# Loads, weight sums and powers of a fused gated block, placed anew

## The chip, the cores and the metric

The kernel runs on one core of a Trainium2 chip. The metric is the device time of one execution in microseconds (us), lower is better. A profile of a single execution shows its span, which is a little shorter than the time. Five engines work side by side, each in the order of its own instructions: TensorE (PE in the profile, PEld for its weight loads), VectorE (DVE), ScalarE (ACT), GpSimd (POOL) and SyncE (SP). SP computes nothing; it issues DMAs.

## The reference

```
x    = x + tanh(g_xattn) * (0.6 * sigmoid(si + sj + b) + 0.4 * layernorm(x))   # si, sj: products of ctx with two rows of W
y    = layernorm(x)
gate = silu(bitlinear(y, w1));  up = bitlinear(y, w2)
x    = x + tanh(g_ffn) * bitlinear(gate * up, w3)

bitlinear(x, w): xn = x * rsqrt(mean(x*x) + 1e-6)
                 xq = round(xn * 127 / max|xn|), scaled back, for each row
                 wq = clip(round(w / mean|w|), -1, 1) * mean|w|
                 xq @ wq.T
```

x is 4 x 512 x 512, ctx 4 x 512 x 128, w1 and w2 are 1408 x 512, w3 is 512 x 1408, all in float32. The mean of |w| runs over a whole weight, so no block of a weight can be rounded before all of it has been read and summed.

## The kernel before, in words

The 2048 rows of x are 16 tiles of 128 rows, numbered 0 to 15, four to each batch. A weight lies in blocks: w1 and w2 in four blocks of 128 x 1408 (704 KB each), w3 in three blocks of 128 x 1536 and one of 128 x 1024. A list of words, `ORDER`, is the program: a loop at the end of the kernel (L576) takes word after word and emits that step. An engine runs its steps in the order of the list, and waits by semaphores for what a step reads and for buffers that it overwrites; nothing reorders them later. So a step that waits holds up all later steps of its own engine, and on SP a DMA that waits holds up every later load, even one that could go at once.

A word is a step's name, a tile or weight number, after a dot the block, and a letter for the engine (a ScalarE, v VectorE, p GpSimd). The steps by their names:

- SP: `x4` loads a tile (tiles 0 to 3) or a pair of tiles, `ctx1` a batch's context, `w1.0` a weight block; `t4` turns an integer 128 x 512 tile with a transposing DMA (L432), `T4` the 128 x 1408 one (L504), `O4` writes a result (L542).
- Attention and first norm: `pi`, `pj` (PE) with `si`, `pjs` (ACT) make the scores; `st` (DVE) statistics, `la`, `lb`, `lc` the layer norm's factors; `th` (ACT) the tanh, `at` (DVE) the sum, `ce` the centring, `am`, `an` (DVE) the largest value and its inverse, `sq` (ACT) the squares, `r` the rounding to int8 range, `dq` (POOL) the factor that undoes it. Tiles 0 to 3 are turned by PE (`pt`), the others by `t`; `un` widens the result to float16, and PE reads that.
- Weights: `A` sums |w| of a block (L241 on ACT, L243 on DVE), `tot` adds the sums over the rows on PE (L247), `M` is the mean (DVE), `R` scales and rounds a block, `C` clips it. `A3.2a` is block 2 of w3 on ACT.
- Products: `G1.0` is tile 1 times block 0 of w1, `U1.0` the same with w2; `G6` does all four blocks. One tile's G, or its U, is 12 matmuls. `SI` (silu, ACT) empties a G, `ST` (DVE) a U. G and U share two PSUM buffers (`ps_gu`), so a product waits for the emptying of the one before the last. `AM`, `AN`, `SQ`, `QU`, `T`, `W` quantize and turn the product, `D` is its product with w3 (11 matmuls), `DQ`, `S`, `O` scale, add and write.
- Small ones: `bp`, `up` spread a scalar parameter over the rows and apply tanh, `cg`, `cc`, `mr`, `os` compute constants of a few values (`mr` is four GpSimd instructions, L480 to L484), `wu5` lets PE run 5 idle matmuls. Small PE results (`pi`, `pj`, `bp`, `tot`, `pt`, `po`) share two other PSUM buffers (`ps_o`).

Before the list starts, ScalarE's own DMA queue gets the attention rows, the first context (`load_ctx(act, 0)`), two scalars, the block w1.3 (`load_w(act, 1, W1_FIRST)`) and the last scalar; then come ScalarE's table load and its first instructions. Inverse square roots are a power of -0.5 on GpSimd, followed by one Newton step (four small instructions, L218 to L221).

Of the kernel before, what the change touches and what calls it, by code (L numbers as in the profile page):

```python
# [32 lines left out]
ORDER = """
x1 bp1 x3 x0 st3 up1 st1 bp0 up0 st0 la0 A1.3a cg lb0p pi0 si0 x2 x4 w1.0 st2 ctx1 st5 pj0 th1 th0
at1 ce1v th3 A1.0a th2 at0 ce0v sq0 x6 w1.2 cc am0 an0 sq1 A1.2a wu5 pi1 si1 la2 lb2p am1 an1 st6
pj1 pjs1 at2 ce2v at3 w1.1 A1.1a w2.2 A2.2a r0p st4 wu4 pt0 wu6 tot1 st7 am2 M1 r1p un0v R1.1v C1.1
R1.0a C1.0 wu3 pt1 R1.2v C1.2 un1a wu6 G1.0 G1.1 G0.0 dq0 w2.3 w2.0 A2.3v G0.1 G1.2 A2.0a w2.1
R1.3p C1.3 A2.1a tot2 an2 ce3a M2 R2.0v R2.2v th6 C2.0 C2.2 R2.1a C2.1 G0.2 G0.3 am3 G1.3 SI1 ctx2
pi2 lc0 pj2 SI0 U1.0 U1.1 U1.2 x8 st9 sq2 th7 la4 lb4p U0.0 U0.1 R2.3p mr at6 C2.3 U1.3 at7 U0.2
U0.3 x10 an3 si2 pjs2 r2p pt2 th5 ce6a ST1 ctx3 pi3 sq3 un2a G2.0 ST0 w3.2 r3p pt3 w3.0 G2.1 G2.2  # L40
G2.3 ce7a am7 sq7 un3a G3.0 G3.1 G3.2 G3.3 A3.0a dq2 lc4 SI2 at5 an7 U2.0 U2.1 U2.2 U2.3 r7p th4
am6 an6 r6p SI3 st8 st11 U3.0 U3.1 U3.2 U3.3 t6 fx1p st10 ce5a si3 at4 ce4v w3.1 sq5 am4 an4 am5
an5 un6v sq4 sq6 bp2 la8 lb8p dq4 ST2 th10 pj3 t7 un7a w3.3 ST3 th11 at11 A3.2a AM2 AN2 G6 SI6 AM1
AM0 th8 r5p AN1 ce11a G7 SI7 U7 ST7 at8 am11 an11 t5 up2 A3.3a r4p U6 ST6 t4 un4a G4 lc8 A3.1a tot3
QU2p QU1p lc2 th9 at9 un5a G5 ce8a T1 SI4 ce9a fx0p W1v T2 at10 ce10v sq9 r11p t11 AN0 un11a U5 SI5
M3 R3.1p sq10 sq8 am10 am9 an9 an10 r10p am8 an8 r9p r8p sq11 dq8 ST5 x12 st13 U4 ST4 t9 un9v R3.3v
C3.3 C3.1 x14 SQ1 st14 st15 pjs3 th13 R3.2p th12 G11 SI11 t8 un8a U11 ST11 st12 R3.0a C3.0 th15 W2v
fx2p QU0p C3.2 os la12 SQ0 lb12p t10 AM6 AN6 QU6p th14 T0 un10v AM3 G9 SI9 at14 ce14v SQ2 fx3a AN3
G8 am14 D1 fx11p SI8 D2 fx6a an14 at15 at12 SQ7 at13 U8 ce13v T6 W0a DQ0 S1 SQ3 QU3v ST8 G10 DQ2
AM4 fx4p ce15a sq15 S2 T3 r14p t14 am13 an13 SI10 D0 r13p t13 AM7 U10 fx7p W6v AN4 QU4p SQ5 U9 S0  # L50
am15 W3a D3 fx9a ST10 ce12a am12 T4 AN7 un13v lc12 fx13v fx14p D6 S3 sq14 un14a G14 O0 sq12 sq13
dq12 ST9 AM10 SQ6 DQ6 W4a SQ4 SI14 QU7p T7 AM5 AN5 SQ10 an15 r15p G13 SI13 D4 U14 AN10 S6 QU5p AM8
U13 T5 AN8 an12 O6 r12p t12 SQ8 W7a D7 fx8a AM9 AN9 QU9v T9 SQ9 ST14 un12v G12 W5v fx15a fx10p O1
DQ4 SQ14 AM14 DQ14 QU8p S4 AN14 QU14v D5 ST13 SQ11 AM11 W9a AN11 S7 U12 SI12 D9 fx5p DQ8 t15 DQ10
un15a S5 G15 ST12 T14 SQ13 QU10v W14a D14 SI15 T8 T10 S9 O9 QU11p AM12 AN12 W8v AM13 T11 AN13 S14
O3 SQ12 U15 D8 W10a D10 QU12p T12 ST15 AM15 QU13p S8 DQ12 AN15 QU15v O14 S10 W11a D11 fx12a T13
W12v D12 W13v T15 O2 O8 S11 O11 O4 O5 O10 SQ15 S12 D13 O12 W15v S13 O7 DQ15 D15 S15 O13 O15
"""


# [1 line left out]
def flamingo_gated_kernel(  # L62
# [72 lines left out]
    def load_ctx(eng, b):  # L135
        eng.dma_start(ctxs[b], ctx_t[:, b * S : (b + 1) * S])

    def load_w(eng, i, k):
        if i < 3:
            eng.dma_start(wf[i][k], (w1t, w2t)[i - 1][k * P : (k + 1) * P, :])  # L140
        else:
            f0, f1 = k * W3S, min((k + 1) * W3S, NH)
            eng.dma_start(
                wf[3][k].rearrange("p (f d) -> p f d", d=D),
                w3t[f0 * P : f1 * P, :].rearrange("(f p) d -> p f d", p=P),
            )
# [10 lines left out]
    mhalf = const.tile([P, TB], F32, name="mhalf")  # L157
# [54 lines left out]
        dve.reciprocal(c_inv, c_sig)  # L212
        dve.scalar_tensor_tensor(c_abs, c_inv, -1.0, c_inv, ALU.mult, ALU.max)

    def newton(eng, r, y, w, n, tag):

        p = small.tile([P, n], F32, tag=f"{tag}_p", name=f"{tag}_p")
        eng.tensor_tensor(p, y, y, ALU.mult)  # L218
        eng.tensor_tensor(p, p, w, ALU.mult)  # L219
        eng.tensor_scalar(p, p, -0.5, 1.5, ALU.mult, ALU.add)  # L220
        eng.tensor_tensor(r, y, p, ALU.mult)  # L221

    def rsqrt(eng, w, n, tag):

        y = small.tile([P, n], F32, tag=f"{tag}_y", name=f"{tag}_y")
        pool.tensor_tensor(y, w, mhalf[:, :n], ALU.pow)
        r = small.tile([P, n], F32, tag=f"{tag}_r", name=f"{tag}_r")
        newton(eng, r, y, w, n, tag)
        return r
# [394 lines left out]
```

## Time and profile before

| | us |
|---|---|
| median of 3 runs (154.28 to 154.74) | 154.52 |
| the profiled execution's own time | 154.62 |
| its span | 152.8 |
| PE busy in the span | 137.5 |
| DVE, ACT, POOL busy | 127.9, 114.2, 101.5 |

The profiled execution is 0.10 us above the median, and 1.8 us of it lie outside the span. A view's times are counted from the span's start. In a view of instructions in order of time, a row gives start, length, engine, line, operation, output and inputs, and in brackets how long the engine was idle before it and what ended that. A row that merges several instructions has their number behind an x.

PE's first product starts at 26.1 us and its last ends at 149.1 us. DMA runs at about 400 GB/s until 31 us, and is then idle for long stretches.

### The profile page before, as it was taken

To read this page: it belongs to the slowest core of one execution; us is meant where nothing else is said; L and a number is where in the kernel's file an instruction comes from. 1 tells how busy PE (TensorE), PEld (TensorE's weight loads), DVE (VectorE), ACT (ScalarE), POOL (GpSimd) and SP (SyncE) were. 2 spreads that over 40 slices of the span, in tenths; PEclk is the share of its full clock that TensorE was granted. 3 is DMA by queue.
4 is the path that set the end of the run, shared out by engine and by line. 5 is a ranking of instruction groups with operands and counts; after the bars stand their busy time and mean duration, and the time that the engine had idled before them with its cause. 6 is when DMAs were issued, how large, how long until landed. Compare 5 with 4: busy or idle time off the path is not lost.

```text
span 152.8 us, 2189 instructions
## 1 busy us (share of the span) xinstructions
PE 137.5 (90%) x659; PEld 67.5 (44%) x659; DVE 127.9 (84%) x226; ACT 114.2 (75%) x167; POOL 101.5 (66%) x214
## 2 busy tenths in 40 slices
PE   5379776799999989999989999999999999999990
PEld 2273433354644434544444444444444444444440
DVE  0384999999999789999899979999995999868521
ACT  0166998879999399999799998888989990928000
POOL 3058473959787865638898978687993788983400
PEclk9999999999999999999999999999999999999998
DMA  5999999940004921672905404351099382599894
GB/s 138 288 417 407 417 417 373 389 180 2 2 0 63 349 42 31 131 186 78 206 0 99 94 0 94 71 101 67 5 193 215 80 166 48 144 178 232 227 381 183
DMA packets 37300, 25.57 MB, mean 167 GB/s; under 512 B 30247, under 2 KB 30248, under 8 KB 37288
## 3 DMA queue, kind: packets, MB, share of 16 engines
q1 hardware_dynamic: 36992, 24.45, 56.5%
q10 hardware_dynamic: 296, 0.98, 2.0%
q8 instruction: 5, 0.08, 0.2%
q14 instruction: 7, 0.06, 0.1%
HBM read 13.89 MB, written 4.19 MB: 118 GB/s over the span
## 4 chain that ended last, share of the span: by engine, by line
DVE 38%; POOL 21%; PE 17%; DMA 12%; issue 6%; ACT 3%; SPq 1%; POOLq 0%; DVEq 0%
PE po L531 12%; DMA x<-in_x_dram 6%; DVE f_am L487 6%; DMA q1t<-q 6%; DVE hs L475 5%; DVE st L346 4%; DVE x L368 4%; DVE am L387 4%; PE pu L463 3%; DVE wk L265 3%; POOL q L499 3%; POOL q L416 3%; POOL x L376 2%; PE pg L463 2%; DVE x L536 1%
## 5 line engine op out<-in xcount | busy, mean ns | idle before, releaser
L463 PEld LDWEIGHTS <-ht 128*128 128x128 f16 x384 | 37.4, 98 | 42.8 <-issue 3.8
L463 PE MATMUL pg<-w1q,ht 128*128 128x512 f16 (+1 forms) x192 | 40.3, 361 | 1.6 <-DVE w1q L268 0.9
L463 PE MATMUL pu<-w2q,ht 128*128 128x512 f16 (+1 forms) x192 | 39.8, 361 | 0.8 <-ACT hs L471 0.7
L531 PE MATMUL po<-w3q,qt 128*128 128x512 f16 x176 | 39.5, 379 | 0.1
L475 DVE SCALAR_TENSOR_TENSOR hs<-pu,a,hs 128x1408 f32<-128x1408 f32 x16 | 26.6, 1673 | 1.7 <-PE pu L463 1.5
L471 ACT ACTIVATE hs<-pg,a 128x1408 f32<-128x1408 f32 x16 | 22.7, 1423 | 5.4 <-PE pg L463 4.2
L531 PEld LDWEIGHTS <-qt 128*128 128x128 f16 x176 | 17.2, 98 | 20.5 <-issue 0.3
L487 DVE TENSOR_REDUCE f_am<-hs 128x1 f32<-128x1409 f32 x16 | 25.6, 1609 | 0.0
L495 ACT ACTIVATE junk<-hs 128x1408 bf16<-128x1408 f32 x16 | 21.9, 1367 | 0.1
L499 POOL TENSOR_SCALAR q<-hs,f_qs 128x1408 int16<-128x1408 f32 x11 | 15.8, 1442 | 4.0 <-DVE f_qs L492 3.6
L346 DVE BATCH_NORM_STATS2 st<-x 128x6 f32<-128x512 f32 x16 | 10.8, 676 | 6.0 <-DMA x<-in_x_dram 6.0
L536 DVE SCALAR_TENSOR_TENSOR x<-po,f_dq,x 128x512 f32<-128x512 f32 x16 | 11.8, 742 | 4.5 <-PE po L531 3.7
L511 ACT ACTIVATE qt<-qtk 128x1408 f16<-128x1408 int16 x8 | 11.0, 1373 | 5.6 <-PE po L531 3.0
L368 DVE SCALAR_TENSOR_TENSOR x<-x,sc,th_all 128x512 f32<-128x512 f32 x16 | 12.1, 766 | 3.6 <-POOL l_p L219 1.9
L387 DVE TENSOR_REDUCE am<-th_all 128x1 f32<-128x513 f32 x16 | 10.7, 674 | 0.1
L399 ACT ACTIVATE junk<-th_all 128x512 bf16<-128x512 f32 x16 | 10.0, 628 | 0.3
L171 PE MATMUL idle<-ones 128*128 128x512 f16 x27 | 8.6, 453 | 1.8 <-POOL ones L166 1.8
L241 ACT ACTIVATE junk<-hs 128x1408 bf16<-128x1408 f32 x7 | 9.6, 1375 | 0.7 <-DMA hs<-in_w1t_dram 0.6
L416 POOL TENSOR_SCALAR q<-th_all,qs 128x512 int16<-128x512 f32 x12 | 8.2, 693 | 1.2 <-DVE qs L396 0.8
L339 ACT ACTIVATE th_all<-ctx,si 128x512 f32<-128x512 f32 x12 | 8.5, 712 | 0.1
L522 POOL TENSOR_SCALAR f_w<-f_ss,kap 128x2 f32<-128x2 f32 (+1 forms) x9 | 3.9, 433 | 5.8 <-ACT junk L495 5.2
L376 POOL TENSOR_SCALAR x<-x,c_sig,sh 128x512 f32<-128x512 f32 x9 | 7.4, 817 | 0.1
(107 smaller groups left out, 180.7 us busy)
## 6 DMA issues: line engine op xcount, KB each, us to landing
out_dram<-x SPq DMA_DIRECT2D x16, 256.0 KB, 2.9
x<-in_x_dram SPq DMA_DIRECT2D x6, 512.0 KB, 7.4
hs<-in_w2t_dram SPq DMA_DIRECT2D x4, 704.0 KB, 11.8
w3f<-in_w3t_dram SPq DMA_DIRECT2D x3, 768.0 KB, 8.8
hs<-in_w1t_dram SPq DMA_DIRECT2D x3, 704.0 KB, 7.4
x<-in_x_dram SPq DMA_DIRECT2D x4, 256.0 KB, 5.0
...
```

The lines of the kernel that those rows point to most:

```text
L346: dve.bn_stats(st, xt(n))
L368: dve.scalar_tensor_tensor(xt(n), xt(n), col(sc, n), ths[n], ALU.mult, ALU.add, accum_out=col(ysum, n))
L387: dve.tensor_reduce(col(am1, n), th_all[:, th_slot[n], : D + 1], AX.X, ALU.max, apply_absolute_value=True)
L416: eng.tensor_scalar(q1s[n], ths[n], col(qs1, n), 127.0 * sign[n], ALU.mult, ALU.mult)
L463: pe.matmul(gus[tag, n][:, c0 : c0 + cn], hts[n][:, kk, :], wq[:, kk, c0 : c0 + cn], start=(kk == 0), stop=(kk == ND - 1),)
L471: act.activation(tts[n], gus.pop(("pg", n))[:, :H], AF.Silu, scale=col(a1, n))
L475: dve.scalar_tensor_tensor(tts[n], gus.pop(("pu", n))[:, :H], col(a1, n), tts[n], ALU.mult, ALU.mult)
L487: dve.tensor_reduce(col(f_am, n), hs[:, t_slot[n], : H + 1], AX.X, ALU.max, apply_absolute_value=True)
L495: act.activation(junk[:, :H], tts[n], AF.Square, accum_out=col(f_ss, n))
L499: eng.tensor_scalar(fq[n], tts[n], col(f_qs, n), 127.0, ALU.mult, ALU.mult)
L531: pe.matmul(po[:, :D], qt[:, f, :], w3q[:, f, :], start=(f == 0), stop=(f == NH - 1))
L536: dve.scalar_tensor_tensor(xt(n), pos.pop(n)[:, :D], col(f_dq, n), xt(n), ALU.mult, ALU.add)
```

## The change

- ScalarE's queue keeps only the attention rows and the three scalars. The first context and block w1.3 move to SP, as `ctx0` (the second load) and `w1.3` (the eleventh). `load_w(act, ...)` and `W1_FIRST` are gone.
- The Newton step is gone from all inverse square roots: `newton` is removed, `rsqrt` is one power on GpSimd. `lb` of the first four tiles goes to VectorE.
- The sum over the last block of w1 and of w2 is made in two halves (`A1.3`, `A1.4`, `A2.3`, `A2.4`), so these weights have five partial sums. Two of w1's are now made on VectorE.
- The clip can be given to an engine; all clips stay on VectorE.
- `ORDER` is new from the first word to the last. Among much else: second and third contexts are loaded ahead of most of w1; the idle matmuls between the first ones and the products go from 24 to 15; most centrings go to GpSimd; tile 2's `G` comes ahead of tile 0's and 1's `U`; the first int8 tile to be turned by DMA is 4 instead of 6, and on SP the loads `x12 w3.1 w3.2 w3.3` stand directly behind `t4`. `A3.2a` and `A3.3a` stand directly ahead of `un4a` on ScalarE.

```diff
 ORDER = """
-x1 bp1 x3 x0 st3 up1 st1 bp0 up0 st0 la0 A1.3a cg lb0p pi0 si0 x2 x4 w1.0 st2 ctx1 st5 pj0 th1 th0
-at1 ce1v th3 A1.0a th2 at0 ce0v sq0 x6 w1.2 cc am0 an0 sq1 A1.2a wu5 pi1 si1 la2 lb2p am1 an1 st6
-pj1 pjs1 at2 ce2v at3 w1.1 A1.1a w2.2 A2.2a r0p st4 wu4 pt0 wu6 tot1 st7 am2 M1 r1p un0v R1.1v C1.1
-R1.0a C1.0 wu3 pt1 R1.2v C1.2 un1a wu6 G1.0 G1.1 G0.0 dq0 w2.3 w2.0 A2.3v G0.1 G1.2 A2.0a w2.1
-R1.3p C1.3 A2.1a tot2 an2 ce3a M2 R2.0v R2.2v th6 C2.0 C2.2 R2.1a C2.1 G0.2 G0.3 am3 G1.3 SI1 ctx2
-pi2 lc0 pj2 SI0 U1.0 U1.1 U1.2 x8 st9 sq2 th7 la4 lb4p U0.0 U0.1 R2.3p mr at6 C2.3 U1.3 at7 U0.2
-U0.3 x10 an3 si2 pjs2 r2p pt2 th5 ce6a ST1 ctx3 pi3 sq3 un2a G2.0 ST0 w3.2 r3p pt3 w3.0 G2.1 G2.2
-G2.3 ce7a am7 sq7 un3a G3.0 G3.1 G3.2 G3.3 A3.0a dq2 lc4 SI2 at5 an7 U2.0 U2.1 U2.2 U2.3 r7p th4
-am6 an6 r6p SI3 st8 st11 U3.0 U3.1 U3.2 U3.3 t6 fx1p st10 ce5a si3 at4 ce4v w3.1 sq5 am4 an4 am5
-an5 un6v sq4 sq6 bp2 la8 lb8p dq4 ST2 th10 pj3 t7 un7a w3.3 ST3 th11 at11 A3.2a AM2 AN2 G6 SI6 AM1
...
+bp1 x1 st1 ctx0 x0 up1 cg st0 x2 st2 cc x3 st3 bp0 w1.0 up0 la0 lb0v ctx1 pi0 si0 pj0 th1 at1 ctx2
+th0 at0 wu5 pi2 th3 la2 lb2v w1.1 w1.2 ce1a th2 at3 am1 ce0p sq1 at2 an1 ce2p am0 an0 ce3p A1.2v
+w1.3 A1.3v A1.0a sq0 r0p si2 A1.1a am2 an2 pi1 si1 pj2 x4 A1.4a wu3 tot1 M1 st4 st5 x6 st6 pjs2
+w2.0 w2.1 w2.2 sq3 sq2 r1p pt1 R1.2a un1v wu1 pj1 R1.0p C1.0v C1.2v R1.1a C1.1v pjs1 th4 wu6 pt0
+un0v th5 A2.1a st7 G1.0 w2.3 A2.0a x14 G1.1 G0.0 G0.1 G0.2 G1.2 dq0 am3 an3 R1.3p C1.3v A2.3a G1.3
+r2v A2.2v la4 lb4p A2.4a ctx3 SI1 pt2 un2v at4 at5 tot2 M2 R2.0v C2.0v G0.3 x8 st9 st8 pi3 x10 st10
+r3p SI0 si3 R2.1a C2.1v R2.2a C2.2v dq2 R2.3p C2.3v th6 st11 at6 G2.0 G2.1 lc2 pt3 G2.2 un3a ce4p
+pj3 G2.3 U1.0 U1.1 U1.2 U1.3 ST1 am4 an4 w3.0 SI2 ce6p am6 mr AM1 A3.0a th7 r4p t4 sq6 ce5p am5 bp2
+up2 G3.0 x12 G3.1 G3.2 G3.3 SI3 pjs3 U0.0 U0.1 U0.2 U0.3 ST0 w3.1 U2.0 U2.1 w3.2 A3.2a la8 w3.3 at7
+ce7p A3.3a lb8p U2.2 U2.3 ST2 U3.0 U3.1 U3.2 U3.3 un4a G4 an6 r6p an5 am7 ST3 sq4 th11 sq7 an7 r5p
+sq5 th8 t6 U4 at8 A3.1a tot3 dq4 at11 SI4 AN1 un6v G6 AM0 t5 ST4 SQ1 th9 AN0 M3 un5a at9 ce8p th10
+at10 ce11p am11 an11 SI6 ce9a am8 sq9 am9 QU1p G5 SI5 ce10a sq10 an8 st12 U6 ST6 lc0 am10 an10 U5
+ST5 r7p r11p R3.0p t7 un7a G7 AM2 sq11 t11 un11a G11 os sq8 QU0p T0 th12 an9 C3.0v r10v T1 th14
...
 """
-    W1_FIRST = 3
-    load_ctx(act, 0)
-    load_param(1)
-    load_param(0)
-    load_w(act, 1, W1_FIRST)
-    load_param(2)
+    for i in (1, 0, 2):
+        load_param(i)
...
-    def newton(eng, r, y, w, n, tag):
...
-    def rsqrt(eng, w, n, tag):
...
+    def rsqrt(r, w):
+
+        pool.tensor_tensor(r, w, mhalf[:, : w.shape[1]], ALU.pow)
...
+    HALVES = ND - 1
     def w_abs(eng, i, k):
         if i not in accs:
-            accs[i] = const.tile([P, len(wf[i])], F32, name=f"acc_{i}")
-        w, acc = wf[i][k], accs[i][:, k : k + 1]
+            accs[i] = const.tile([P, len(wf[i]) + (i < 3)], F32, name=f"acc_{i}")
+        w, acc = wf[i][min(k, HALVES)], accs[i][:, k : k + 1]
+        if i < 3 and k >= HALVES:
+            h = w.shape[1] // 2
+            w = w[:, :h] if k == HALVES else w[:, h:]
...
-    def w_clip(i, k):
-        dve.tensor_scalar(wd[i][k], wks.pop((i, k)), 1.0, -1.0, ALU.min, ALU.max)
+    def w_clip(eng, i, k):
+        eng.tensor_scalar(wd[i][k], wks.pop((i, k)), 1.0, -1.0, ALU.min, ALU.max)
...
-        pool.tensor_tensor(lny[:, cols], lnw[:, cols], mhalf[:, :n], ALU.pow)
+        rsqrt(rst[:, cols], lnw[:, cols])
...
-        newton(eng, rst[:, cols], lny[:, cols], lnw[:, cols], n, f"l{n}")
...
-        r = rsqrt(pool, vw, n, f"v{n}")
+        r = small.tile([P, n], F32, tag=f"vr{n}", name=f"vr_{n0}")
+        rsqrt(r, vw)
...
-        r = rsqrt(pool, f_w[:, cols], n, "f")
+        r = small.tile([P, n], F32, tag=f"fr{n}", name=f"fr_{n0}")
+        rsqrt(r, f_w[:, cols])
```

More of the change, by code (lines that the diff above doesn't have):

```diff
@@ L39 @@
-pi2 lc0 pj2 SI0 U1.0 U1.1 U1.2 x8 st9 sq2 th7 la4 lb4p U0.0 U0.1 R2.3p mr at6 C2.3 U1.3 at7 U0.2
-U0.3 x10 an3 si2 pjs2 r2p pt2 th5 ce6a ST1 ctx3 pi3 sq3 un2a G2.0 ST0 w3.2 r3p pt3 w3.0 G2.1 G2.2
-G2.3 ce7a am7 sq7 un3a G3.0 G3.1 G3.2 G3.3 A3.0a dq2 lc4 SI2 at5 an7 U2.0 U2.1 U2.2 U2.3 r7p th4
-am6 an6 r6p SI3 st8 st11 U3.0 U3.1 U3.2 U3.3 t6 fx1p st10 ce5a si3 at4 ce4v w3.1 sq5 am4 an4 am5
-an5 un6v sq4 sq6 bp2 la8 lb8p dq4 ST2 th10 pj3 t7 un7a w3.3 ST3 th11 at11 A3.2a AM2 AN2 G6 SI6 AM1
-AM0 th8 r5p AN1 ce11a G7 SI7 U7 ST7 at8 am11 an11 t5 up2 A3.3a r4p U6 ST6 t4 un4a G4 lc8 A3.1a tot3
@@ L45 @@
[L45 to L55, printed above, removed]
@@ L56 @@
-O3 SQ12 U15 D8 W10a D10 QU12p T12 ST15 AM15 QU13p S8 DQ12 AN15 QU15v O14 S10 W11a D11 fx12a T13
-W12v D12 W13v T15 O2 O8 S11 O11 O4 O5 O10 SQ15 S12 D13 O12 W15v S13 O7 DQ15 D15 S15 O13 O15
+bp1 x1 st1 ctx0 x0 up1 cg st0 x2 st2 cc x3 st3 bp0 w1.0 up0 la0 lb0v ctx1 pi0 si0 pj0 th1 at1 ctx2
+th0 at0 wu5 pi2 th3 la2 lb2v w1.1 w1.2 ce1a th2 at3 am1 ce0p sq1 at2 an1 ce2p am0 an0 ce3p A1.2v
+w1.3 A1.3v A1.0a sq0 r0p si2 A1.1a am2 an2 pi1 si1 pj2 x4 A1.4a wu3 tot1 M1 st4 st5 x6 st6 pjs2
+w2.0 w2.1 w2.2 sq3 sq2 r1p pt1 R1.2a un1v wu1 pj1 R1.0p C1.0v C1.2v R1.1a C1.1v pjs1 th4 wu6 pt0
@@ new lines @@
+ce7p A3.3a lb8p U2.2 U2.3 ST2 U3.0 U3.1 U3.2 U3.3 un4a G4 an6 r6p an5 am7 ST3 sq4 th11 sq7 an7 r5p
+sq5 th8 t6 U4 at8 A3.1a tot3 dq4 at11 SI4 AN1 un6v G6 AM0 t5 ST4 SQ1 th9 AN0 M3 un5a at9 ce8p th10
+at10 ce11p am11 an11 SI6 ce9a am8 sq9 am9 QU1p G5 SI5 ce10a sq10 an8 st12 U6 ST6 lc0 am10 an10 U5
+ST5 r7p r11p R3.0p t7 un7a G7 AM2 sq11 t11 un11a G11 os sq8 QU0p T0 th12 an9 C3.0v r10v T1 th14
+fx2a SI7 r9v U11 R3.1p C3.1v st13 lc8 R3.2a W0v dq8 SI11 r8p st14 W1a U7 st15 R3.3p C3.3v C3.2v D0
+t10 th13 AN2 ST11 un10a t9 ST7 SQ0 un9a G9 fx9a SQ2 lc4 fx6a QU2p fx3p fx0a AM3 AN3 la12 lb12p at14
@@ new lines @@
+t8 at12 un8a T2 W2a AM5 DQ0 AM4 ce14p AN5 QU3p SI9 fx1p D1 S1 th15 am14 at15 G8 SI8 fx4p T3 W3a AN4
+at13 ce13v ce12v sq12 fx11a QU5p S0 SQ3 SQ6 T5 am13 an13 U8 ST8 AM8 QU4p T4 SQ4 r13p sq13 AN8 U9 D2
+QU8p am12 an14 an12 DQ2 sq14 G10 D3 SI10 ST9 AM9 SQ9 AN9 S2 U10 t13 un13a r12p W4v D4 ST10 ce15p
+AM7 sq15 t12 am15 fx5a an15 O2 r14p t14 W5a G13 AM6 QU9p S3 dq12 un14a G14 T8 lc12 AN6 D5 QU6v AM10
+SQ7 O3 SQ8 AN10 SQ5 SI13 T6 SI14 fx15a fx10a un12v r15p t15 DQ4 S4 U14 fx14p W8v D8 DQ8 QU10p fx8p
@@ L58 @@
+DQ6 ST14 AM14 SQ11 AN14 S5 U13 T9 S8 O4 AN7 QU7p QU14v W6a O8 W9a AM11 SQ10 SQ14 D6 S6 O1 ST13 DQ14
+AM13 T7 W7a D9 G12 SI12 O5 un15v T10 S9 O0 U12 ST12 SQ12 D7 DQ10 AM12 AN12 AN11 QU11v O6 G15 SI15
+AN13 U15 fx7v S7 SQ13 W10v D10 T14 W14v D14 T11 W11a ST15 AM15 AN15 S10 S14 QU12p T12 W12a QU15v
+QU13p T13 O9 D11 S11 fx13a T15 W13v fx12a DQ12 D12 S12 O14 O10 D13 O12 W15v S13 O11 O13 SQ15 DQ15
+D15 S15 O7 O15
 """
@@ L213, in gate_constants @@
         dve.scalar_tensor_tensor(c_abs, c_inv, -1.0, c_inv, ALU.mult, ALU.max)
-    def newton(eng, r, y, w, n, tag):
[L217 to L221, printed above, removed]
-    def rsqrt(eng, w, n, tag):
[L225 to L229, printed above, removed]
+    def rsqrt(r, w):
+        pool.tensor_tensor(r, w, mhalf[:, : w.shape[1]], ALU.pow)
     junk = const.tile([P, W3S * D], BF16, name="junk")
+    HALVES = ND - 1
     accs, tots, mean, inv, wks = {}, {}, {}, {}, {}
@@ L245, in w_total @@
     def w_total(i):
-        tots[i] = ps_o.tile([P, 512], F32, tag="po", name=f"tot_{i}")[:, : len(wf[i])]
+        tots[i] = ps_o.tile([P, 512], F32, tag="po", name=f"tot_{i}")[:, : accs[i].shape[1]]
         pe.matmul(tots[i], ones, accs[i], start=True, stop=True)
@@ L297, in flamingo_gated_kernel @@
     lnw = const.tile(NTT, F32, name="lnw")
-    lny = const.tile(NTT, F32, name="lny")
     sc = const.tile(NTT, F32, name="sc")
@@ L565, in flamingo_gated_kernel @@
         "A": w_abs, "tot": no_k(w_total), "M": no_k(w_mean), "R": w_round,
-        "C": lambda eng, n, k: w_clip(n, k),
+        "C": w_clip,
         "G": lambda eng, n, k: product(n, k, w1q, "pg"),
```

## The prediction

> **What bounds the kernel now.** I read the page's forty slices first, then the matmuls in order of time, then SP's queue and what it waited for, then DMA traffic microsecond by microsecond.
>
> ```profile
> PE   5379776799999989999989999999999999999990
> ...
> ACT  0166998879999399999799998888989990928000
> ...
> GB/s 138 288 417 407 417 417 373 389 180 2 2 0 63 349 42 31 131 186 78 206 0 99 94 0 94 71 101 67 5 193 215 80 166 48 144 178 232 227 381 183
> ```
>
> PE is full from the eighth slice to the end. G or U of one tile takes 2.38 us (12 matmuls), D 2.37, so 48 such units are 114 us; they run from 26.1 to 149.1, which leaves 5 us of small matmuls and 4 us of waits. So time is won by starting earlier, and lost by any PE wait after that. The head, in order of time over all engines:
>
> ```profile
> 7.01 1.28 ACT L162 ACT_TABLE_LOAD   x1 [7.01 <-DMA ctx<-in_ctx_t_dram]
> ...
> 9.24 1.87 PE L316 MATMUL pi<-wc,ctx 128*128 128x1 f32 x8
> ...
> 13.12 1.84 ACT L339 ACTIVATE th_all<-pj,si 128x512 f32<-128x512 f32 x3 [1.38 <-PE pj L323]
> ...
> 23.32 0.15 DVE L252 TENSOR_REDUCE mean<-tot 128x1 f32<-128x4 f32 x1
> ```
>
> ScalarE's queue holds its engine until 7.0, scores wait for that, tanh for the scores; w1's mean is done at 23.9. Then the middle, PE first:
>
> ```profile
> 45.07 4.92 PE L463 MATMUL pu<-w2q,ht 128*128 128x512 f16 x24
> 49.91 0.38 PE L187 MATMUL spread<-row,ones 1*128 1x1 f32 x2
> ...
> 51.18 4.92 PE L463 MATMUL pg<-w1q,ht 128*128 128x512 f16 x24
> ```
>
> At 51.18 the G and U of tiles 0 to 3, eight units, and all small matmuls but `tot3` are done, and the ninth unit starts. SP, in order of time, and its longest wait:
>
> ```profile
> 20.08 2.69 SPq L143 DMA_DIRECT2D w3f<-in_w3t_dram  x2
> 45.42 1.28 SPq L432 DMA_TRANSPOSE q1t<-q  x1
> 46.75 0.57 SPq L143 DMA_DIRECT2D w3f<-in_w3t_dram  x1
> 47.37 1.20 SPq L432 DMA_TRANSPOSE q1t<-q  x1
> 48.61 0.60 SPq L143 DMA_DIRECT2D w3f<-in_w3t_dram  x1
> ```
>
> ```profile
> SPq L432 <- POOL x L376: 23.6, 2, 22.6
> ```
>
> This is the row to remember: SP stood 22.6 us at `t6`, which waited for its rounded tile, and `w3.1` behind it, whose buffer was free, went out only at 46.75. DMA meanwhile moved nothing. How fast a load then comes (stretch; busy time of PE, PEld, DVE, ACT, POOL; clock, DMA share, GB/s):
>
> ```profile
> 48.00:49.00 1.00, 1.00 (x7) 0.49 (x5) 0.93 (x5) 0.94 (x5) 0.72 (x4) 1.00 0.63 12
> 49.00:50.00 1.00, 1.00 (x7) 0.38 (x4) 1.00 (x2) 1.00 (x3) 0.54 (x2) 1.00 0.57 221
> 50.00:51.00 1.00, 1.00 (x4) 0.60 (x5) 1.00 (x2) 0.22 (x1) 0.94 (x1) 1.00 1.07 418
> ```
>
> Behind a transpose the bulk flows 2.3 us after the load's issue (46.75 to about 49), then at up to 418 GB/s. Before, this hurts nobody: w3's last sums run at 59 to 62 us.
>
> **The change, part by part.**
>
> *Queues.* ScalarE issues four small rows (0.23 to 0.51 us each) and is free at about 2.3 instead of 7.0. The page has no row for a scalar's landing without a context ahead of it: the attention row landed within 2.5 us, `g_xattn` took 4.2 behind the context. By the first, `up1` is done at 5.2, by the second at 6.5; I take 5.2. Context 0, now second on SP, lands at 5 to 6.7; the loads that moved to SP are 1.0 MB, but the bytes up to the last of w1 fall from 5.5 to 4.7 MB, since x4 and x6 now come later: at 415 GB/s 1.9 us sooner, about 16.5 to 17.4, ahead of the sums that read it. Context 0 passes x0, x2 and x3 on SP: 0.6 us of issue and as much transfer for each of them, hidden, since `cg` (1.16) stands ahead of their statistics on DVE; without that, 0.6 on the path. Scores then start at 5.6 and tanh, 3.9 us later as now, at 10 (I give half a us away).
>
> *Head.* From tanh on, by rows: DVE does `lb at1 at0 lb at3 am1 at2 an1 am0 an0` (at 0.70, am 0.62, an 0.35) to 15.6, then a whole sum (1.55) and half of one (0.8) to 18.1. ACT does three more tanh and a centring (0.62 each), two squares (0.72), two sums (1.47) and the last half (0.85) to 18.7. The mean comes at 19.65, 4.2 earlier. GpSimd's and ACT's roundings (1.7 and 1.45) with DVE's clips (0.48) start G1.0 at 22.95 (-3.1); G1 and G0 follow as their clips come, the last at 26.6. `tot2` then blocks PE from 27.8 to 30.1, behind ACT's four sums for w2 (25.1 to 29.9). G2 needs the buffer that `SI1` empties at 31.2, U1 the clips of w2, the last at 36.5. U1 ends at 37.6; `bp2`, then G3, U0, U2, U3 (4 x 2.38) follow after a short wait for `SI2`, to 47.6. That is 3.6 us ahead of 51.18, with the same eight units and small matmuls done.
>
> *Newton, halves, centrings.* Newton's 4 instructions (0.20 to 0.26 us and 0.08 between) go from 19 powers: 21 us of GpSimd, of which only the ones in `la0`, `dq0` lie in the head (counted above); the rest was hidden beside PE. GpSimd gets 11 centrings; the nearest row is its L416, 0.69 us each, so 7.6 us back, hidden too while it has this slack; without it they would delay `r`. DVE gets 4.6 us lighter (5 fewer centrings, 4 fewer roundings, against two more sums, three `r`), ACT 1.2 heavier. Whether GpSimd disturbs DVE: one DVE rounding took 2.14 instead of 0.95 beside one on GpSimd. I take 0, the upper end is 1 us. The extra partial sum costs one accumulator read (0.19), counted above, and one more column in `tot`: nothing. The clip's engine letter changes nothing, and `lb` on DVE is one instruction of 0.2, counted.
>
> *The loads behind `t4`.* New SP order: `w3.0 t4 x12 w3.1 w3.2 w3.3 t6`. `t4` waits for `r4`, on GpSimd behind `ce6p` and `mr` (2.5 us in the trace), and for `an4`, on DVE behind `ST1`. U1 ends 37.6; `ST1` to 39.6, `am4`, `an4` to 40.4; `ce6p` to 38.7, `mr` to 41.2, `r4` to 41.9. So T = 41.9 for `t4`'s issue, and not before 40.7 by DVE's side alone. `x12` is issued at T+1.3; bulk from T+3.6; x12, w3.1, w3.2 are 2.1 MB, 5.05 us: w3.2 is there at 50.5, w3.3 at 51.8. ACT comes to `A3.2a` at 42.9 and stands until 50.5; then `A3.2a` (1.57), `A3.3a` (1.13), `un4a` (0.52): 53.8. PE's next unit, G4, needs `un4a`, while PE is done at 47.6: a wait of 6.2 us. DVE, behind `at8` (whose tanh is queued on ACT), waits too.
>
> Here a rule is weighed. The Trainium skill, page "DMA: Bandwidth & Descriptors", section "Anatomy of one DMA", gives a fit of 2.0 us plus bytes over 436 GB/s, made for GpSimd's issuing path, and says that a DMA's semaphore wait happens on the sequencer that issues it. SP's 22.6 us agree with the second; the first makes w3.2 land at 41.9+1.3+2.0+4.8 = 50.0, half a us sooner than the row; I take the row, as it stands behind a transpose.
>
> A second rule speaks against the change. Clock: the profile's idle matmuls (L171) take 634 ns each up to 14.9 us and 379 ns from 17.9 on. The Trainium skill, "TensorE: Matmul & The Clock Gate", section "Part 1: The HAM clock gate", says that about 3.4 us of idleness halve PE's clock again, and as much work restores it. Before, no PE wait after 20 us reaches even 1.5. With 6.2 us of idleness G4 could take up to 1.7 us longer. By the rows alone: 0. Either way it is nearly free, because G6 waits for ACT's `SI4` behind `A3.1a`, at 60.1, whereas U4 ends at 58.6 (cold 60.3). I add 0. Fewer idle matmuls ahead of G1 (24 to 15) leave gaps under 1.5 us: 0 too; if cold, 1.7 at most, mostly under `tot2`'s wait.
>
> *The rest.* From 53.8 ACT does `sq4 th11 sq7 sq5 th8 A3.1a SI4` (0.72 a square, 0.62 a tanh, 1.57, 1.33) to 60.1, so G6 starts there; G5 waits for `un5a`, 62.7, then without a gap to the 18th unit's end at 79.4. Before, it ended at 76.35. So +3.05. The 30 units left are the same work in both; before they hold 1.0 us of waits, and with GpSimd and DVE lighter I take off 0.35 (0 to 1.0). The end is alike: six D, 14.2 us, after U15, and 3.7 us from the last matmul to the end. Sum: +3.05 - 0.35 = +2.7. Profile 154.62 + 2.7 = 157.3; against the median, 0.10 lower, 157.2.
>
> **The rivals.**
>
> *The load is in time (faster).* If w3.2 and w3.3 come before ACT needs them, the head's 3.6 us stay: 150.9. If ACT stands half as long, about 153. It decides at `A3.3a`: G4 at 51.2 is break-even, so w3.3 must be there by 49.5, T at 39.6 or before. For it: loads might start without the 2.3 us behind a transpose; `mr` might be shorter. Against it: `an4` alone keeps T at 40.7. A head 1.5 us earlier than I count would do it as well. 16%, and 6% for landing within 0.3% of no change, which is what a measurement of this kernel can tell apart.
>
> *The head gains little (slower still).* ScalarE's small rows may land as late as now (`g_xattn` at 5.87), SP's first loads may come alone no faster than now (6.2), and contention costs 1 us: then the head gains 1.5 instead of 3.6 and the stall stays: 159.5. Also here: the change doesn't free ScalarE early. 12%.
>
> *The forecast:* ACT's wait eats more than the head gave: 157.2, on its own 155.2 to 159.5. 66%.
>
> **How the numbers follow.** Slower 0.66 + 0.12 = 0.78, same 0.06, faster 0.16. About one in ten lies below 153.0 and one in ten above 160.3.
>
> **What would show it.** First product at 23 us; ScalarE's table load before 4; four small GpSimd instructions fewer behind each power. The main sign: ACT idle for 5 to 8 us before L241 with `w3f`, released by DMA, about 43 to 51 us, SP's `x`/`w3f` issues right behind the first transpose, and a PE wait of 4 to 7 us before G4 released by ACT L439's line for widening. I am wrong if that wait is under 3 us, or if G1 starts after 25.

## The result, and the profile after

The changed kernel takes 165.73 us (median of 4 runs, 163.72 to 166.67), the kernel before 154.40 (median of 4, 153.82 to 154.74): ratio 1.0694, 95% interval 1.059 to 1.0799. Slower was forecast, but 157.2 and not over 160.3. The profiled execution took 165.47, its span is 163.4. One remark on spread: where a kernel has runs more than 1.5% above its fastest one, which is so for after and for the fourth and the sixth experiment, the ratio leaves these out and the median counts all (without them the three medians are 165.47, 152.41 and 162.30).

Of the page of after, the rows that answer to those of before (forty slices of 4.1 us, busy tenths; PEclk is the granted clock):

```profile
PE   5994899979963199999999995999989999987990
...
ACT  3269999997600998899999748988999553616600
...
PEclk9997559999999759999999999999999999999999
...
GB/s 112 311 415 412 422 424 401 270 0 0 8 265 353 82 32 4 0 64 176 65 50 75 10 166 89 32 47 171 100 105 138 158 306 123 0 70 111 289 251 150
```

ACT has work from the first slice on, which it had not before, and later two empty slices at 45 to 53 us; PE's hole follows, mostly at 50 to 57 us. PEclk, 9 throughout before, falls to half twice: at about 14 to 25 us, and behind that hole. DMA stands still at 33 to 45 us, while SP waits at `t4` with w3's blocks behind it.

The head of after, rows of ScalarE, PE and VectorE in order of time:

```profile
2.10 1.28 ACT L159 ACT_TABLE_LOAD   x1 [2.10 <-issue]
...
5.59 1.84 PE L304 MATMUL pi<-wc,ctx 128*128 128x1 f32 x8 [0.21 <-ACT par L192]
...
9.45 1.84 ACT L327 ACTIVATE th_all<-pj,si 128x512 f32<-128x512 f32 x3 [1.65 <-PE pj L311]
...
19.60 0.16 DVE L244 RECIPROCAL inv<-mean 128x1 f32<-128x1 f32 x1
...
22.35 2.54 PE L168 MATMUL idle<-ones 128*128 128x512 f16 x6
...
24.96 4.32 PE L451 MATMUL pg<-w1q,ht 128*128 128x512 f16 x21
```

Up to the mean this is the forecast to within about half a us: scores 5.59 (5.6), tanh 9.45 (10), mean 19.76 (19.65). Then the first product comes at 24.96, not 22.95. The six idle matmuls ahead of it take 2.54 us together, at half clock, and `pj1` ahead of these (at 20.65) 1.91. Before, six took 1.46:

```profile
23.74 1.46 PE L171 MATMUL idle<-ones 128*128 128x512 f16 x6
```

In the sixth experiment the same six take 1.46 and `pj1` 1.02. The difference, 1.97 us, is as much as the lateness.

The middle of after, PE in order of time:

```profile
47.83 2.54 PE L451 MATMUL pu<-w2q,ht 128*128 128x512 f16 x12 [1.53 <-DVE hs L463]
56.50 4.87 PE L451 MATMUL pg<-w1q,ht 128*128 128x512 f16 x12 [6.13 <-ACT ht L427]
```

SP's queue there, and ACT's longest wait by the view of waits (total, times, longest):

```profile
43.51 1.28 SPq L420 DMA_TRANSPOSE q1t<-q  x1
44.84 0.57 SPq L130 DMA_DIRECT2D x<-in_x_dram  x1
45.45 1.56 SPq L143 DMA_DIRECT2D w3f<-in_w3t_dram  x3
```

```profile
ACT junk L230 <- DMA w3f<-in_w3t_dram: 9.0, 1, 9.0
```

This is the stall that the prediction named: `x12` and three blocks of w3 leave right behind `t4`, ACT stands 9.0 us at `A3.2a` (7.6 expected), and PE 6.13 us (6.2) before G4. So the mechanism is there at its size. It doesn't explain 8.5 us more than forecast: in the profiled execution G4 is 2.7 us later than forecast, G6 4.0, and the end of the last product 7.8 (159.6 against 149.1 + 2.7). The groups of after show what does, first of all:

```profile
L371 POOL TENSOR_SCALAR th_all<-x,ysum 128x512 f32<-128x512 f32 x11 | 22.0, 2000 | 5.6 <-DVE x L355 3.0
```

GpSimd's centring takes 2.00 us, where I had put 0.69. Late in the kernel PE has waits that the kernel before has not:

```profile
101.83 2.54 PE L451 MATMUL pg<-w1q,ht 128*128 128x512 f16 x12 [1.89 <-DVE hs L463]
...
149.94 9.67 PE L520 MATMUL po<-w3q,qt 128*128 128x512 f16 x44 [1.10 <-ACT qt L499]
```

### The profile page after: what moved, and what is told of

Its sections match the earlier page's. It is cut to its first block, busy times and chain, and to the rows that moved or that the text cites. A ratio compares the mean times of both kernels' runs of the same rounds, so it can differ in the third digit from the quotient of the medians.

```text
span 163.4 us, 2099 instructions
## 1 busy us (share of the span) xinstructions
PE 141.2 (86%) x650; PEld 68.4 (42%) x650; DVE 128.2 (78%) x222; ACT 116.3 (71%) x168; POOL 99.9 (61%) x143
## 4 chain that ended last, share of the span: by engine, by line
PE 34%; DVE 24%; ACT 15%; POOL 11%; issue 6%; DMA 6%; SPq 1%; DVEq 0%; ACTq 0%; POOLq 0%
PE po L520 10%; PE pu L451 9%; PE pg L451 7%; ACT junk L483 5%; DMA w3f<-in_w3t_dram 4%; ACT junk L230 4%; POOL th_all L371 4%; DVE hs L463 3%; DVE f_am L475 3%; PE idle L168 3%; DVE st L334 3%; PE pj L311 2%; ACT junk L386 2%; DVE x L355 2%; DVE x L525 2%
## 5 line engine op out<-in xcount | busy, mean ns | idle before, releaser
L451 PE MATMUL pg<-w1q,ht 128*128 128x512 f16 (+1 forms) x192 | 42.8, 376 | 8.0 <-ACT ht L427 6.1
L451 PE MATMUL pu<-w2q,ht 128*128 128x512 f16 (+1 forms) x192 | 40.7, 364 | 3.2 <-DVE hs L463 1.5
L487 POOL TENSOR_SCALAR q<-hs,f_qs 128x1408 int16<-128x1408 f32 x12 | 18.3, 1525 | 19.7 <-DVE f_qs L480 9.4
L520 PEld LDWEIGHTS <-qt 128*128 128x128 f16 x176 | 17.0, 98 | 22.6 <-ACT qt L499 1.6
L371 POOL TENSOR_SCALAR th_all<-x,ysum 128x512 f32<-128x512 f32 x11 | 22.0, 2000 | 5.6 <-DVE x L355 3.0
L483 ACT ACTIVATE junk<-hs 128x1408 bf16<-128x1408 f32 x16 | 21.9, 1369 | 2.9 <-DVE hs L463 2.7
L499 ACT ACTIVATE qt<-qtk 128x1408 f16<-128x1408 int16 x9 | 12.1, 1369 | 9.5 <-DMA qtk<-q 4.8
L355 DVE SCALAR_TENSOR_TENSOR x<-x,sc,th_all 128x512 f32<-128x512 f32 x16 | 13.0, 835 | 7.5 <-ACT th_all L327 7.4
L230 ACT ACTIVATE junk<-w3f 128x1536 bf16<-128x1536 f32 (+1 forms) x4 | 5.5, 1375 | 9.0 <-DMA w3f<-in_w3t_dram 9.0
L311 PE MATMUL pj<-ctx,wc 128*128 128x512 f32 x8 | 7.1, 981 | 2.0 <-ACT si L316 2.0
L404 POOL TENSOR_SCALAR q<-th_all,qs 128x512 int16<-128x512 f32 x10 | 6.9, 690 | 2.5 <-DVE qs L383 2.2
```

The costliest lines, as they stand in the source:

```text
L355: dve.scalar_tensor_tensor(xt(n), xt(n), col(sc, n), ths[n], ALU.mult, ALU.add, accum_out=col(ysum, n))
L371: eng.tensor_scalar(ths[n], xt(n), UP, col(ysum, n), ALU.mult, ALU.subtract)
L451: pe.matmul(gus[tag, n][:, c0 : c0 + cn], hts[n][:, kk, :], wq[:, kk, c0 : c0 + cn], start=(kk == 0), stop=(kk == ND - 1),)
L483: act.activation(junk[:, :H], tts[n], AF.Square, accum_out=col(f_ss, n))
L487: eng.tensor_scalar(fq[n], tts[n], col(f_qs, n), 127.0, ALU.mult, ALU.mult)
L520: pe.matmul(po[:, :D], qt[:, f, :], w3q[:, f, :], start=(f == 0), stop=(f == NH - 1))
```

## The experiments

Three suspects: the stall on w3 (theory A), the centrings at 2.0 us (theory B), and later TensorE's clock in the head. The first four kernels ran beside a kernel before of 154.77 us (7 runs), the next four beside 154.56 (7), the last three beside 154.85 (7). Each change is made to the kernel after unless it says otherwise.

**1. Loads first.** w3's blocks no longer stand behind `t4`:

```
- ... am4 an4 w3.0 SI2 ... t4 ... ST0 w3.1 U2.0 U2.1 w3.2 A3.2a la8 w3.3 at7
+ ... am4 an4 w3.0 w3.1 w3.2 w3.3 SI2 ... t4 ... ST0 U2.0 U2.1 A3.2a la8 at7
```

> The changed kernel with w3.1, w3.2 and w3.3 issued right behind w3.0, ahead of t4; x12 stays behind t4. Theory A (w3's blocks stuck behind t4 on SP are the main cost): ACT's 9.0 us wait at A3.2a is gone, PE's wait before G4 falls from 6.1 to under 1 us, PE's clock is not halved there, and 7 to 9 us go: 157 to 159 us. Theory B (GpSimd's centrings at 2.0 us instead of 0.69 are the main cost): DVE, ACT and PE go on waiting for them, at most 3 us go: 163 or more.

Measured: 158.05 us (157.52 to 158.69), ratio 1.0199 (1.0143 to 1.0256), 7.7 less than after. ACT's wait for w3 and PE's before G4 are gone; PE's first product and G4 in this kernel:

```profile
22.63 4.59 PE L451 MATMUL pg<-w1q,ht 128*128 128x512 f16 x21
...
48.45 2.54 PE L451 MATMUL pg<-w1q,ht 128*128 128x512 f16 x12
```

So the stall is a main cost of after, as A has it. But without it the kernel is still slower than before, so it isn't the only one.

**2. GpSimd centres with an add.** x times -512 plus the row's sum, with the sign carried along as ScalarE's centrings do already:

```
-        sign[n] = -1.0 if eng is act else 1.0
+        sign[n] = 1.0 if eng is dve else -1.0
...
+        elif eng is pool:
+            eng.tensor_scalar(ths[n], xt(n), -UP, col(ysum, n), ALU.mult, ALU.add)
```

> The changed kernel with GpSimd's centring written as -512 x + sum (multiply, add) with the sign turned, as ACT does it, instead of 512 x - sum (multiply, subtract); SP's order untouched. If the subtraction is what costs 2.0 us, the instruction falls to about 0.77 as L363 (multiply, add); if it is the operand or the place, it stays at 2.0. Theory A: ACT's wait for w3.2 stays above 7 us and 1 to 4 us go: 161.5 to 164.5. Theory B: 7 us or more go: 158 or less.

Measured: 161.35 us (160.47 to 162.0), ratio 1.0407 (1.0346 to 1.0467), 4.4 less than after. The group of the centrings in this kernel:

```profile
L371 POOL TENSOR_SCALAR th_all<-x,ysum 128x512 f32<-128x512 f32 x11 | 7.6, 698 | 8.2 <-DVE x L355 3.4
```

Eleven at 698 ns, with the same input, output and place: 14.4 us of GpSimd's time were the form of the instruction. Both suspects count.

**3. Clock kept up ahead of G4.** 27 idle matmuls, into an output buffer of their own, between U3 and G4:

```
- ... U3.0 U3.1 U3.2 U3.3 un4a G4
+ ... U3.0 U3.1 U3.2 U3.3 kw un4a G4      # kw: 27 idle matmuls
```

> The changed kernel with 27 idle matmuls on PE between U3 and G4, in PE's wait (5.8 us when warm). The wait stays; only PE's clock differs. If the halved clock after it costs time: G4 takes 2.4 instead of 4.9 us, U4 2.4 instead of 2.8, and 2 to 3 us go: 162.5 to 163.5. If, as the prediction had it, the slow G4 is hidden behind ACT's SI4: G4 is fast, but the time is the same within 0.7 us.

Measured: 164.94 us (164.25 to 165.32), ratio 1.0628 (1.0563 to 1.0694); 0.8 less than after. PE of this kernel:

```profile
56.68 2.55 PE L451 MATMUL pg<-w1q,ht 128*128 128x512 f16 x12 [0.38 <-ACT ht L427]
59.07 2.54 PE L451 MATMUL pu<-w2q,ht 128*128 128x512 f16 x12
...
63.40 4.88 PE L451 MATMUL pg<-w1q,ht 128*128 128x512 f16 x23 [1.66 <-ACT hs L459]
```

G4 takes 2.55 instead of 4.87, and then G6 waits 1.66 for ACT's `SI4`. It starts at 63.40 instead of 64.14. So the clock behind the stall was worth some 0.7 us; the prediction's claim that `SI4` hides it holds for most of it.

**4. Loads first and add together.**

> Loads ahead of t4 and GpSimd's centring by addition together. Theory A: about the first run's time less 1 to 3 us, 154 to 157. Theory B: the second run's time less 2 or so. If both are costs of their own and add up: near 154, the kernel before. If the head's gain comes through at last: 151 to 152.

Measured: 154.13 us as the median of 151.93, 152.89, 155.38 and 156.12; ratio 0.9833 (0.9756 to 0.9911). The profiled execution was the slowest of these. Its clock row, and PE at `tot2`:

```profile
PEclk9997589956999999999999999999999999999999
```

```profile
30.05 0.39 PE L236 MATMUL tot<-acc,ones 128*128 128x5 f32 x2 [1.77 <-ACT junk L230]
30.29 1.32 PE L453 MATMUL pg<-w1q,ht 128*128 128x512 f16 x3
31.41 1.71 PE L304 MATMUL pi<-wc,ctx 128*128 128x1 f32 x8
```

Here three matmuls of `G0.3` take 1.32 us and `pi3` 1.71; in the kernel after, at full clock, they take 0.76 and 0.95. The clock falls in the head, where the change cut the idle matmuls from 24 to 15. That made a third theory: part of after's loss, and of the spread here, is the clock in the head. In this execution PE had also waited 2.05 us for a context, at 12.67, which could be a rival cause of the spread; no faster execution of this kernel was profiled.

**5. Loads first, add, and a busy head.** 17 more idle matmuls, only where PE waits anyway:

```
- wu5 pi2 ... si1 pj2 ... un1v wu1 pj1 ... at4 at5 tot2
+ wu7 pi2 ... si1 wu5 pj2 ... un1v wu3 pj1 ... at4 at5 kw tot2      # kw: 8 idle matmuls
```

> The kernel after with three things changed: w3's four loads stand together ahead of t4, GpSimd centres by multiply and add, and TensorE gets 17 more idle matmuls in the head (2 behind the first five, 5 ahead of pj2, 2 ahead of pj1, 8 between pt2 and tot2), which fill waits only. Theory A (the spread of the kernel with the first two things, 151.9 to 156.1, is TensorE's clock halved after waits of 1.8 to 2 us in the head): every run now lies within 151 and 152.7, no slice of the clock row before 40 us is under 9, G1.0 starts at 22.6 to 23.2, and G2 and U1 run at 2.4 each. Theory B (the clock there does not depend on such waits, or the slow runs come from late loads of the context): the spread stays, with runs at 155 and above, and the extra matmuls cost up to 1 us. A clear gain over the kernel before: ratio 0.98 to 0.99.

Measured: 150.49 us (150.29 to 151.52), ratio 0.975 (0.9714 to 0.9786). All four runs lie within 1.3 us; 4.2 us was the spread of experiment 4. That the idle matmuls narrowed it is not shown, for experiments 1 and 2, also without them, spread by only 1.2 and 1.5. The page's rows of this kernel, and its G4:

```profile
PE   5999899999999999999999989999999999999990
...
PEclk9999599999999999999999999999999999999999
```

```profile
22.76 4.60 PE L453 MATMUL pg<-w1q,ht 128*128 128x512 f16 x21
...
46.74 2.54 PE L453 MATMUL pg<-w1q,ht 128*128 128x512 f16 x12
```

One slice, at 15 to 18.5 us, still has a low clock, which my expectation excluded, but behind it the clock is full. G1 starts at 22.76 (the prediction said 22.95), U3 ends and G4 starts at 46.74 (47.6), with no wait. This version beats the kernel before by 4.1 us, and is what the change could have been: the forecast's case of loads that come in time, 150.9.

**6. After with the busy head alone.**

> The kernel after with the same 17 idle matmuls in the head and nothing else. Theory A: of the 2 us by which G1.0 came later than I had forecast (24.96 against 22.95) most is TensorE's clock; G1.0 starts at 22.6 to 23.5, but the stall of ACT on w3 sets G4 and takes most of it back, since t4 waits for r4 behind GpSimd's centrings at 2.0 us: 164.0 to 165.5. Theory B (head's lead passes through in full): 163.2 to 163.8. Theory C (the clock in the head is not the cause): 165.2 to 166.5, G1.0 at 24.5 or later.

Measured: 162.78 us (162.25 to 164.87), ratio 1.052 (1.0483 to 1.0558); 2.95 less than after. Its PE:

```profile
23.02 4.32 PE L451 MATMUL pg<-w1q,ht 128*128 128x512 f16 x21
...
54.97 4.30 PE L451 MATMUL pg<-w1q,ht 128*128 128x512 f16 x12 [6.14 <-ACT ht L427]
```

G1 starts 1.94 earlier than in after, G4 1.53 earlier, behind the same wait. The clock is the cause of the late first product, by the lengths of `pj1` and of the six idle matmuls, and the lead passes the stall almost in full, for the stall starts when `t4` goes out and that too comes 1.5 earlier. This is even more than theory B expected; of the rest, some 1.4, most comes at the end, where the wait of 1.10 ahead of the last four D is absent. That is not the head's clock. The wait stands, with 1.10 to 1.54 us, in the traces of all four kernels without `kw` (after, experiments 1, 2 and 4) and in none of the six with it, experiment 3 among them, where `kw` stands ahead of G4 and the head is as in after. `kw` takes one more turn of the two `ps_o` buffers; how that ends the wait no run shows.

Nor do the traces show that the idle matmuls keep the clock up. Without them G1 starts at 22.63, 22.82 and 23.46 in experiments 1, 2 and 4, and late, at 25.05, only in experiment 3; with them it starts at 22.76, 22.87 and 23.70 in experiments 5, 7 and 8, but late in experiment 9, where `pj1` is slow again:

```profile
21.56 1.71 PE L311 MATMUL pj<-ctx,wc 128*128 128x512 f32 x2
...
24.63 4.32 PE L453 MATMUL pg<-w1q,ht 128*128 128x512 f16 x21
```

So a slow clock just ahead of G1 costs about 2 us in the executions that meet it, and whether one does is not settled by these 17 matmuls alone.

**7 and 8. The two others, each alone, with the busy head.** Loads first, with the centrings left at 2.0 us:

> The kernel after with w3's loads together ahead of t4 and the 17 idle matmuls, but GpSimd's centrings left as multiply and subtract (2.0 us each). Beside the kernel with all three edits (150.5) it gives the price of the centrings alone. Theory A (they cost TensorE waits early and in the last 30 units, some 4 us, as they seemed to with the load stall in place): 154 to 155.5, with a PE wait of about 1.5 behind VectorE ahead of U3 and of about 2 near 90 us. Theory B (without the load stall GpSimd has slack again): 151 to 152.5.

Add, with the loads left behind `t4`:

> The kernel after with GpSimd's centrings as multiply and add and the 17 idle matmuls, but w3's blocks left behind t4. Beside the kernel with all three edits (150.5) it gives the price of the load stall alone, with head and centrings as the prediction had them. Theory A (the stall and its working are right: 157.2): 157 to 159, with ACT waiting 7 to 9 us on w3 and PE 6 to 7. Theory B (the centrings' 2 us held r4, and so t4, and made the stall): t4 goes out over 1.5 us earlier than in the kernel after and the stall costs under 4 us: 153 to 154.5.

Measured: loads first 157.17 us (155.85 to 157.68), ratio 1.0128 (1.0065 to 1.019), 1.7 above what I expected at most; add 160.05 us (158.98 to 160.49), ratio 1.0309 (1.0246 to 1.0371), 1.1 above. With experiments 5 and 6 this makes a square at the same head (medians, us):

| | centring by subtract | centring by add |
|---|---|---|
| w3 behind `t4` | 162.78 | 160.05 |
| w3 ahead of `t4` | 157.17 | 150.49 |

The stall costs 5.6 with the slow centrings and 9.6 without them; the centrings cost 2.7 beside the stall and 6.7 without it. Each hides some 3 to 4 us of the other (3 if each kernel is taken against the kernel before of its own group). After and experiments 1, 2 and 4 make the same square without the busy head: there the stall costs 7.7 and 7.2, the centrings 4.4 and 3.9, and nothing is hidden. But in that square the head's clock is mixed in: it was low ahead of G1 in after and from 30 us in experiment 4, and at neither place in the two others. These two differ from experiments 7 and 8 by the busy head alone, which is worth 0.9 and 1.3 us there, about what the wait ahead of the last four D took in the two (1.54 and 1.10). In both squares the centrings cost time without the stall. So theory B's hope that GpSimd has slack once the stall is gone is wrong. How a GpSimd instruction gets onto the path is seen in PE of loads first with the slow centrings:

```profile
45.91 2.54 PE L451 MATMUL pu<-w2q,ht 128*128 128x512 f16 x12 [1.54 <-DVE hs L463]
...
92.59 4.22 PE L451 MATMUL pg<-w1q,ht 128*128 128x512 f16 x12 [2.09 <-DVE hs L463]
```

The first wait: `am5` stands in VectorE's order ahead of `ST0` and waits for `ce5p` on GpSimd, so `ST0` is late, which must empty a product's buffer before U3 can have it. Ahead of the second, VectorE had waited 1.31 us for a scaled tile from GpSimd, which stood there behind a centring and a rounding. It costs twice, because the clock falls behind it: 4.22 for twelve matmuls.

**9. Is it the subtract?** Experiment 2 changed the operation and the constant's sign. Here the constant stays at -512 and the operation is a subtract again, so the row's sum goes in with the wrong sign and only the times can be read:

```
-            eng.tensor_scalar(ths[n], xt(n), -UP, col(ysum, n), ALU.mult, ALU.add)
+            eng.tensor_scalar(ths[n], xt(n), -UP, col(ysum, n), ALU.mult, ALU.subtract)
```

> The kernel with all three edits, with GpSimd's centring as x times -512 minus the row's sum, in place of plus: the centring takes the sum off with the wrong sign, so that part of the computation is changed, and only the instruction's time is read. Theory A (the subtract is what takes 2 us): eleven instructions at 2.0 us, and the time near that of the kernel with the two other edits alone. Theory B (the negative constant or the place in the order made it 0.70): they stay at 0.70.

Measured: one run of 157.58 us, within the runs of the seventh experiment, and

```profile
L371 POOL TENSOR_SCALAR th_all<-x,ysum 128x512 f32<-128x512 f32 x11 | 22.0, 2003 | 5.8 <-DVE x L355 3.2
```

It is the subtract.

**10. The kernel before with Newton's step taken out,** and nothing else:

```
-        y = small.tile(...); pool.tensor_tensor(y, w, mhalf[:, :n], ALU.pow)
-        newton(eng, r, y, w, n, tag)
+        pool.tensor_tensor(r, w, mhalf[:, : w.shape[1]], ALU.pow)
```

> The kernel before with Newton's step taken out of all 19 powers and nothing else: some 21 us of GpSimd's time go. By the prediction's working this is hidden beside TensorE but for one in the head, where lb0p stands ahead of at1: 153.9 to 154.7. Rival (GpSimd's chain lies on the path, as r waits for it in the last 30 units): 152.5 to 153.7. Second rival (an earlier GpSimd disturbs VectorE): 155 or more.

Measured: 153.51 us (153.42 to 153.84), ratio 0.9939 (0.9918 to 0.996), 1.05 less than its before; not "hidden", but in its rival's range, though not in the last 30 units where the rival had it. Most of it lies in one place. ACT in order of time, the widening of tile 6, which stood at 52.70 in the kernel before:

```profile
51.57 0.63 ACT L427 ACTIVATE ht<-q1t 128x512 f16<-128x512 int16 x1 [1.30 <-DMA q1t<-q]
```

`r6` comes earlier on GpSimd, so `t6`, the transpose for which SP stood 22.6 us in before, goes out earlier, ACT is 1.1 us earlier, and a wait of PE behind ACT is gone. It is this one of the kernel before:

```profile
56.78 5.08 PE L463 MATMUL pu<-w2q,ht 128*128 128x512 f16 x24 [0.68 <-ACT hs L471]
```

Another 0.5 are small gaps that the kernel before has at 117 to 123 us.

**11. The kernel before with Newton out and only small rows on ScalarE's queue,** its own order kept but for three places:

```
-    load_ctx(act, 0); load_param(1); load_param(0); load_w(act, 1, W1_FIRST); load_param(2)
+    for i in (1, 0, 2): load_param(i)
- x1 bp1 ... la0 A1.3a cg ... at1 ce1v th3 A1.0a
+ x1 ctx0 bp1 ... la0 w1.3 cg ... at1 ce1v th3 A1.3a A1.0a
```

> The kernel before with its own order of steps, and only two parts of the change: ScalarE's queue carries the four small rows alone (context 0 second on SyncE's queue, w1's last block on SyncE's queue ahead of x2, its sum on ScalarE moved behind th3, as it would now be waited for), and Newton's step is gone. Theory A (the early ScalarE is what the head gains from): scores at about 5.6, tanh at 9.5 to 10, w1's mean 1.9 earlier (the tanh comes 3.4 earlier, the moved sum takes 1.57 of it), G1.0 at 24.2, and the lead is kept to the end: 152.4 to 153.6. Theory B (a later wait takes the lead back: a clip, w2's sums, SyncE's queue behind t6): 154.0 to 155.

Measured: 151.85 us (151.29 to 152.68), ratio 0.9829 (0.979 to 0.9868). Its first product:

```profile
24.36 3.37 PE L447 MATMUL pg<-w1q,ht 128*128 128x512 f16 x15 [0.85 <-DVE w1q L252]
```

24.36 against 24.2 expected, and the lead is kept to the end: the free ScalarE gives 1.66 beside Newton's 1.05. These two parts of the change help; what loses lies in the rest of it, and experiments 1, 2 and 6 say where. The sums in halves were not tried alone.

## Why the prediction was right and wrong

Right was the direction and its reason: the load behind `t4`, ACT's wait, PE's wait of 6.1 to 6.2 before G4, and a head that is earlier by the early ScalarE. Wrong was the size. The steps that failed are the price of GpSimd's centrings, taken from a row of another operation, and two terms put at or near 0, the clock behind the missing idle matmuls and the waits in the last 30 units. From the forecast to the measurement by the medians, each step with one thing that the sum had otherwise:

| | us |
|---|---|
| forecast | 157.2 |
| measured with centrings at 0.70 and a busy head (experiment 8) | 160.05 |
| with centrings at 2.0 (experiment 6) | 162.78 |
| with the head as it is in after | 165.73 |

The size of a step depends on the order in which they are taken, as the square shows, and the runs of one kernel here spread by 1.5 to 3 us, so a step is known to about 1 us. The last step also holds the wait of 1.10 that goes with `kw`.

- **"The nearest row is its L416, 0.69 us each, so 7.6 us back, hidden":** 22.0 us, and not hidden; +2.7 here. The nearest row had the same shape and engine, but multiplies twice and writes int16. A nearer one, L376 (multiply and add, fp32 in and out, 0.82 us), would have said no more: the trace of before has no subtract on GpSimd, and I gave no upper end for it; VectorE's centring (L384, 545 ns) is a subtract too and tells nothing about GpSimd.
- **"Fewer idle matmuls ahead of G1 leave gaps under 1.5 us: 0 too; if cold, 1.7 at most, mostly under `tot2`'s wait":** PE stood 2.02 us ahead of `pj2` at 15.60, and the cold clock cost 1.9 at G1 and 1.5 at G4. The bound was about right for its place; that it would be hidden, and that the value is 0, was wrong. The 2.3 us at `tot2` that were to cover it were 0.35 in after. That the missing idle matmuls are what let the clock fall stays open: in experiment 1 the same 2.02 us ahead of `pj2` were followed by a full clock at G1.
- **The load.** In experiment 8, head and centrings are near the forecast (scores 1.0 late, but U3's end only 0.2). SP, ACT's wait, and DMA by the microsecond (columns as before):

```profile
41.43 1.29 SPq L422 DMA_TRANSPOSE q1t<-q  x1
...
50.96 1.48 ACT L230 ACTIVATE junk<-w3f 128x1536 bf16<-128x1536 f32 x1 [8.31 <-DMA w3f<-in_w3t_dram]
```

```profile
46.00:47.00 1.00, 1.00 (x7) 0.49 (x5) 1.00 (x1) 0.00 (x0) 0.72 (x2) 1.00 1.01 387
47.00:48.00 1.00, 0.82 (x5) 0.20 (x3) 0.97 (x5) 0.00 (x0) 0.64 (x1) 1.00 1.05 346
48.00:49.00 1.00, 0.00 (x0) 0.00 (x0) 1.00 (x1) 0.00 (x0) 0.72 (x2) 1.00 0.92 328
```

  `t4` went out at 41.43 (41.9 forecast) and w3.2 came 9.5 later, not 8.6, as the loads ran at 330 to 390 GB/s and not at 415. `w3.3` then cost another 0.38, and G4 started at 54.64 (53.8): +0.8. In experiment 6 the issue at 41.9 to 42 was right by two errors that cancel: `mr` took 1.25 us on GpSimd instead of 2.5, the centring ahead of it 2.0 instead of 0.7. The fit from the Trainium skill, page "DMA: Bandwidth & Descriptors", section "Anatomy of one DMA", weighed in the prediction, erred further in the same direction: it put w3.2 8.1 behind the issue.
- **ACT from there to `SI4`:** in experiment 8, `SI4` waited 0.61 for GpSimd's `dq4`, which the sum did not have. G6 started at 61.35, not 60.1; +0.4 beside the 0.8 above.
- **"The 30 units left are the same work; I take off 0.35":** PE's waits in them were 1.8 us in experiment 8 (0.42, 0.76, 0.65) and 4.3 in after (1.89, 0.68, 0.65, 1.10), where I had 0.65. The steps stand in a new order, so the waits of before say little about those of after. It was the least argued term and cost 1.2 even with the other causes gone.
- **Newton "hidden":** 1.05 us was on the path, by way of `r6`, `t6` and ACT.
- **Clock behind the stall, "I add 0":** right to some 0.7 us.

Of the rivals, that the load is in time (150.9) is what happens when w3's blocks stand ahead of `t4` and the two other things are mended: 150.49. That it is so close is in part luck: G4 starts 0.9 earlier than forecast, and the waits behind it are 1.4 (0.43, 0.35, 0.66), not 0.65. The head gaining 1.5 instead of 3.6 (159.5) is near to what the clock did, but the cause I gave there, late small rows, was wrong: they came as forecast.
